# Keys of the last layer: 49 block products for four batches at a time, laid between the heads

## The chip, the core and the metric

The kernel runs on one core of a Trainium2 chip, in float32. A core has a matrix engine (TensorE, PE in the profile; its weight loads are listed as PEld), a vector engine (DVE), an activation engine (ACT), a general engine (POOL), and a queue (SP) from which this kernel issues its DMAs. Matmuls write to PSUM, eight banks of 128 partitions by 512 floats; DVE and ACT read PSUM, POOL doesn't. The metric is the device time of one execution in microseconds: 2974.27 us in the median of three runs before the change (2973.41 to 2974.33).

## The reference

Four layers work on x (8 batches of 112 tokens, 512 channels), with a context of 8 batches of 375 tokens.

```
x = L0(x, ctx)   # one cross-attention, width 512
x = L1(x, ctx)   # RWKV block: time mix with a scan over the 112 tokens, channel mix
x = L2(x, ctx)   # the same form with other weights
x = L3(x, ctx, ctx):
    h = layer_norm(x);  x = x + cross_attention_1(h, ctx)   # 16 heads of 128
    h = layer_norm(x);  x = x + cross_attention_2(h, ctx)
    return x + gelu(layer_norm(x) @ w_fc1 + b_fc1) @ w_fc2 + b_fc2

cross_attention: q = h @ wq + bq;  k = ctx @ wk + bk;  v = ctx @ wv + bv
    k, v = [k; bias_k], [v; bias_v]        # 376 keys per batch
    out = softmax(q k^T / sqrt(128)) v @ wo + bo
```

The change concerns `k = ctx @ wk` of the last layer: 375 tokens of eight batches, 512 channels in, 16 x 128 out, in each of two attentions.

## The kernel before, in words

**Products by seven.** Large products are done by a scheme of seven block products for a 2 x 2 block matrix, where the plain way has eight. It needs sums and differences of the blocks of both factors beforehand and of the products afterwards. The seven are called k1, k2, k5, k6, k7, k8, k9. For the weights the sums are made by POOL (`weight_sums`, L1021 to L1038: four instructions of 512 columns for a 512 x 512 weight). For the context they are made once in layer 0 (`park`) and stored in DRAM as `blocks`: for each pair of batches seven combinations of two batches and two channel halves.

**Values and early keys in the scans.** The values of the last layer don't depend on x, so they are computed during layers 1 and 2, by the generator `values` (L820). It is a sequence of pieces, each a block product of two matmuls with its evacuation; `fill(n)` runs the next n pieces wherever it stands in the code of layers 1 and 2: in layer norms, and once or twice per step of the scan (L688, L697). Four sets of 48 units in all give the values of both attentions; a fifth set of three units (L831) gives the keys of attention 1, groups 1 and 2, batches 0 and 1: 56 matmuls of 125 columns a unit. Results go to DRAM (`store`, L913). Between sets, `relay` (L852) replaces the seven weight blocks step by step, some by DMA, some by POOL, while the last unit of the old set and the first units of the new one run; `after` (L957) lets a step go when a named piece and two more have been made. Inside the scans the order of the instructions of PE, DVE, ACT and POOL is the order in which they are written (`manual_schedule`, L679). Everywhere else, and on the SP queue, a planner orders each engine's instructions by its own costs, in program order where several are ready.

**Channel mix** (`channel_mix`, L720): layer norm, a shifted difference (POOL, L359), two mixed inputs xk and xr (DVE, L738), three projections fk, fr, fv with evacuation by ACT (L753, L763) or DVE (L769), and the addition to x by POOL (L770). In layer 2 the call at L731 runs all pieces that are left.

**The last layer** (`attention`, L1166). The 16 heads are taken in four groups of four. For each group the queries come from a product by seven (`project7`, `seven`, L1047); then for each of eight batches and each head of the group: scores (L1289), softmax (`softmax`, L212: maximum by DVE, exponential by ACT, scaling by DVE at L220), three transposes (L1292), and per batch the product with the values (L1302) and the addition of the bias (L1309). The output projection of the group is again a product by seven. Two PSUM banks (`mm`) hold products, two (`sc`) scores, three transposes, one the context.

**The keys before** (`key_pieces`, `chained`, L1176 and L1105). Before batches 0, 2, 4, 6 of a group the keys of that batch and the next are made: seven products, in two halves of the outputs, each of two accumulating matmuls of 375 columns. That is 28 matmuls and 14 evacuations per pair of batches. They alternate between two banks. Each pair loads its context and four combinations anew. In the first group of an attention the pieces of batches 0 to 3 also fill the layer norm before (`first_keys`, L1206); there the additions are POOL's, elsewhere DVE's (L1140, L1142). Of 32 pairs of batch and group in both attentions, 30 are made so, and two come from the early keys.

**Between groups** four pieces of the output projection, four of the next queries, and the rest follow each other (`some`, L1258).

Of the kernel before, what the change touches and what calls it, by code (L numbers as in the profile page):

```python
# [22 lines left out]
F32 = mybir.dt.float32  # L23
# [6 lines left out]
P = 128  # L30
B, L, C, S = 8, 112, 512, 375
N = B * L
# [16 lines left out]
BLOCK = 2 * CT  # L49

# [58 lines left out]
def tile_kernel(ctx: ExitStack, tc: tile.TileContext, d: dict, out: bass.AP):  # L109
# [14 lines left out]
    def weight(name, g=None):  # L124

        w = wpool.tile([P, NC, C], F32, tag="w", name=f"w_{name}_{g}")
        nc.sync.dma_start(w, d[name] if g is None else d[name][g])
        return w
# [421 lines left out]
    def time_mix(n, pre, center_h, pick, k, v, r, g, decay, rows):  # L550
# [8 lines left out]
        with (  # L559
# [119 lines left out]
            with tc.manual_schedule(engines=ORDERED):  # L679
                vp = led(0)  # L680
                for c in range(NC):
                    side = beside(c)
                    for at, j in enumerate(order):
# [13 lines left out]
                        fill(int(at not in (6, 10)))  # L697
# [22 lines left out]
    def channel_mix(n, pre, names, first):  # L720
        nonlocal filler
        with (
# [11 lines left out]
            def mixed(maa, name):  # L734
                y = one.tile([P, NC, N], F32, name=name)
# [13 lines left out]
            rr = one.tile([P, NC, N], F32, name=f"rr{n}")  # L749
# [6 lines left out]
            xk = mixed(names["fk"], f"xk2_{n}")  # L756
            project(ps, f_k, lambda c, h: halves(xk[:, c, :], h), squared, f"fk{n}")
            xr = mixed(names["fr"], f"xr2_{n}")
# [20 lines left out]
            else:  # L779

                for _ in values_pieces(0):
# [3 lines left out]
                y, sq = (  # L785
                    wpool.tile([P, NC, C], F32, tag="w", name=f"{what}_ln3")[:, :, :NH] for what in ("y", "sq")
# [4 lines left out]
                shared["normed"] = y  # L791

# [27 lines left out]
    def values():  # L820
# [6 lines left out]

        pre = "L3_xattn_"
        pool, spill, ps = shared["pool"], shared["spill"], shared["ps"]
        sets = [("wv", i, (gr, gr + 1)) for i in (1, 2) for gr in (0, 2)] + [("wk", 1, (1, 2))]  # L830
        units = [(at, unit) for at in range(len(sets)) for unit in range(UNITS if at < 4 else 3)]  # L831
# [20 lines left out]
        def relay(at, old, new):  # L852
# [8 lines left out]
            yield "k1"  # L861
            nc.gpsimd.tensor_sub(old["k1"], a11, a21)
            yield "k5"
            nc.gpsimd.tensor_add(a21, a21, a22)
            yield "k9"
            nc.gpsimd.tensor_sub(old["k6"], a21, a11)
            yield "k7"
            raw(old["k7"], at, 0, 1)
            yield "k8"
            raw(old["k8"], at, 1, 1)  # L870
            yield "k5"
            raw(old["k5"], at, 0, 0)
            new["k1"] = old["k5"]
            yield "k6"
            nc.gpsimd.tensor_sub(old["k2"], old["k7"], old["k6"])
            yield "k9"
            nc.gpsimd.tensor_copy(old["k9"], a21)
# [19 lines left out]
        def product(p, t, s, start=True):  # L897

            if len(p.shape) == 2:
                todo = [(p, t[k], s[:, k], k) for k in range(2)]  # L900
            else:
                todo = [(p[:, o], s[:, k, o * P : (o + 1) * P], t[k][:, :CT], k) for o in range(HG) for k in range(2)]

            for n, (to, left, right, k) in enumerate(todo):
                nc.tensor.matmul(to, left, right, start=start and n == 0, stop=k == 1, skip_group_check=True)  # L905

        def shaped(y, f):
# [602 lines left out]
```

## Time and profile before

| what | us |
|---|---|
| median of three runs | 2974.27 |
| the profiled execution | 2975.13 |
| its span, first to last instruction | 2972.9 |
| PE busy | 2865.5 |
| DVE, ACT, POOL busy | 1608.9, 999.1, 876.6 |

The mean granted clock of PE was 0.986. In time: layer 0 to about 160 us, layer 1 to 790 (its scan from 363), layer 2 to 1441 (its scan from 982), attention 1 to about 2094, attention 2 to 2790, then the MLP. "Busy" is the time in which an engine runs at least one instruction. In a group's line "<-" stands between the tile that is written and those that are read; "[1.30 <-ACT k L1136]" behind a timeline row says that the engine was idle for 1.30 us before it, and that ACT's instruction on line 1136 ended that. A float32 matmul is recorded as two passes, so it counts as two.

### The profile page before, as it was taken

What the parts mean: (1) busy time and instruction counts of PE and PEld (TensorE: products, weight loads), DVE (VectorE), ACT (ScalarE), POOL (GpSimd) and SP (SyncE); (2) the same over time, 40 slices, a digit from 0 to 9 for tenths busy, and PEclk for the clock granted to TensorE, in tenths of its full rate; (3) what the DMA queues carried; (4) which work ended last, traced back from release to release, by engine and by line L of the source; (5) the groups of instructions that cost most, each with busy time, mean ns of one, the idle gap of its engine ahead of it and who ended that gap; (6) DMA issues with size and microseconds to landing.
All of it is one profiled execution on the core that took longest, in us unless ns stands there. A gap on an engine that the chain in (4) does not pass through costs nothing.

```text
span 2972.9 us, 29802 instructions
## 1 busy us (share of the span) xinstructions
PE 2865.5 (96%) x10130; PEld 1561.6 (53%) x10130; DVE 1608.9 (54%) x2350; ACT 999.1 (34%) x1992; POOL 876.6 (29%) x702
## 2 busy tenths in 40 slices
PE   8989999999999999999899999999999999999999
PEld 4734443344444433356466666666565666656544
DVE  1563288857342687743445454545555454545455
ACT  2123355533233455532332222223331323323311
POOL 2142078754231587732411010100302010000030
PEclk9989999999999999999999999999999999999999
DMA  7421398944321888742344343334233433432110
GB/s 255 150 89 45 116 294 248 275 135 127 95 66 57 254 244 263 225 143 70 130 125 133 118 139 114 122 109 149 88 114 100 151 107 119 140 104 87 39 57 25
DMA packets 199318, 402.90 MB, mean 136 GB/s; under 512 B 33288, under 2 KB 119592, under 8 KB 192384
## 3 DMA queue, kind: packets, MB, share of 16 engines
q1 hardware_dynamic: 199168, 401.01, 43.1%
q8 instruction: 81, 1.33, 0.2%
q14 instruction: 69, 0.57, 0.1%
HBM read 323.16 MB, written 77.91 MB: 135 GB/s over the span
## 4 chain that ended last, share of the span: by engine, by line
PE 80%; DVE 8%; POOL 4%; DMA 3%; ACT 3%; issue 2%; SPq 0%; DVEq 0%; POOLq 0%; ACTq 0%
PE ps_vk L905 13%; PE ps_k1k L1133 10%; PE ps_k5k L1133 7%; PE av L1302 6%; PE sc L1289 5%; PE ps_o L161 3%; PE pt L1292 3%; PE ps_k1q L1060 2%; PE ps_r L484 2%; PE ps_k L484 2%; PE ps_k5q L1060 2%; PE ps_fr L161 2%; PE ps_k7q L1060 2%; PE ps_fk L161 2%; PE ps_k7fc L1060 1%
## 5 line engine op out<-in xcount | busy, mean ns | idle before, releaser
L905 PE MATMUL ps_vk<-wv,cv 128*128 128x512 f32 x1336 | 602.9, 602 | 31.4 <-DMA wv<-in_L_xattn_wv 12.7
L905 PEld LDWEIGHTS ps_vk<-wv,cv 128*128 128x128 f32 x1336 | 251.4, 192 | 366.9 <-issue 306.9
L931 POOL TENSOR_TENSOR k<-k,k 128x512 f32<-128x512 f32 (+1 forms) x153 | 202.1, 1321 | 308.1 <-ACT k L930 261.3
L691 DVE TENSOR_TENSOR_SCAN st<-decay,kv 128x904 f32<-128x904 f32 x128 | 260.7, 2037 | 16.5 <-POOL rs L695 3.8
L695 POOL TENSOR_TENSOR rs<-st,r 128x896 f32<-128x896 f32 x128 | 246.6, 1927 | 55.6 <-DVE st L691 46.6
L218 ACT ACTIVATE prob<-sc,top 112x376 f32<-112x376 f32 (+1 forms) x264 | 151.8, 575 | 322.8 <-DVE top L215 195.3
L1289 PE MATMUL sc<-k,q 128*112 128x376 f32 x512 | 201.1, 485 | 0.7 <-ACT prob L218 0.7
L1302 PEld LDWEIGHTS av<-pts,v 125*128 125x128 f32 (+1 forms) x1536 | 185.0, 193 | 31.4 <-DVE pts L1298 16.3
L1282 POOL COPY k<-over_k 128x4 f32<-128x4 f32 x64 | 13.8, 224 | 604.7 <-PE sc L1289 576.7
L1302 PE MATMUL av<-pts,v 125*128 125x112 f32 (+1 forms) x1536 | 189.1, 277 | 2.1 <-DVE pts L1298 2.0
L1133 PE MATMUL ps_k1k<-cs,wsk 128*128 128x375 f32 x480 | 179.8, 483 | 1.5 <-ACT p1k L1136 1.5
L687 DVE TENSOR_TENSOR kv<-vp,k 128x904 f32<-128x904 f32 x128 | 141.5, 1105 | 70.3 <-ACT vp L589 64.8
L215 DVE TENSOR_REDUCE top<-sc 112x1 f32<-112x376 f32 (+1 forms) x264 | 143.4, 544 | 64.4 <-PE sc L1289 51.9
L930 ACT COPY k<-ps_vk 128x512 f32<-128x512 f32 (+1 forms) x153 | 89.2, 583 | 183.1 <-PE ps_vk L905 180.1
L998 ACT COPY k<-ps_vk 128x512 f32<-128x512 f32 (+1 forms) x153 | 89.1, 582 | 157.6 <-PE ps_vk L905 151.7
L1292 PEld LDWEIGHTS pt<-ident_l,prob 112*125 112x125 f32 (+1 forms) x768 | 97.9, 176 | 73.0 <-DVE prob L220 43.9
L1292 PE MATMUL pt<-ident_l,prob 112*125 112x112 f32 (+1 forms) x768 | 121.2, 277 | 3.3 <-DVE prob L220 2.1
L220 DVE TENSOR_SCALAR prob<-prob,total 112x376 f32<-112x376 f32 (+1 forms) x264 | 118.3, 449 | 8.0
L1133 PEld LDWEIGHTS ps_k1k<-cs,wsk 128*128 128x128 f32 x480 | 90.0, 191 | 60.1 <-issue 2.4
L1140 DVE TENSOR_TENSOR k<-ps_k5k,u2k 128x375 f32<-128x375 f32 x52 | 28.5, 549 | 159.2 <-PE ps_k5k L1133 158.2
L589 ACT COPY vp<-vj 128x896 f32<-128x896 f32 x124 | 112.8, 910 | 4.4 <-DMA vj<-rows 0.4
L1309 DVE TENSOR_TENSOR ctxt<-av,bv 128x448 f32<-128x448 f32 x64 | 40.0, 625 | 128.3 <-PE av L1302 128.2
(384 smaller groups left out, 4792.2 us busy)
## 6 DMA issues: line engine op xcount, KB each, us to landing
vj<-rows SPq DMA_DIRECT2D x124, 448.0 KB
cv<-blocks SPq DMA_DIRECT2D x181, 251.5 KB
cs<-blocks SPq DMA_DIRECT2D x120, 375.0 KB
wvs<-k SPq DMA_DIRECT2D x128, 256.0 KB
v<-wvs SPq DMA_DIRECT2D x64, 512.0 KB
cx<-in_ctxT SPq DMA_DIRECT2D x38, 750.0 KB
v<-wvs SPq DMA_DIRECT2D x64, 252.0 KB
wvs<-k SPq DMA_DIRECT2D x64, 224.0 KB
```

What stands on the lines that cost most here:

```text
L161: nc.tensor.matmul(p, w[:, k, o * P : (o + 1) * P], rhs(k, h), start=k == 0, stop=k == NC - 1)
L215: nc.vector.tensor_reduce(top, scores, AX.X, ALU.max, negate=True)
L218: nc.scalar.activation(prob, scores, AF.Exp, bias=top, accum_out=total)
L691: nc.vector.tensor_tensor_scan(flat(st), flat(decay[:, c]), flat(kv), 0.0, ALU.mult, ALU.add)
L695: nc.gpsimd.tensor_mul(by_batch(rs), st[:, :, :L], by_batch(r[:, c, :]))
L905: nc.tensor.matmul(to, left, right, start=start and n == 0, stop=k == 1, skip_group_check=True)
L931: nc.gpsimd.tensor_add(y, z, y)
L1060: nc.tensor.matmul(to, lhsT, rhs, start=start and k == 0, stop=k == 1, skip_group_check=not start)
L1133: nc.tensor.matmul(y, lhsT, rhs, start=start and k == 0, stop=k == 1, skip_group_check=True)
L1289: nc.tensor.matmul(sc, q[:, o, tok], kt[:, o, :], start=True, stop=True)
L1292: nc.tensor.transpose(pt[t][:nt, o, :], prob[:, t0 : t0 + nt], ident[:L, :L])
L1302: nc.tensor.matmul(av[:, o, :], v[:nt, t, o * HD : (o + 1) * HD], pts[:nt, t, o, :], start=t == 0, stop=t == 2,)
```

## The change

1. The fifth set of `values` goes; its sets hold values alone. In `relay` each step now names its own lag: three loads are issued right after the piece that frees their slot, and the first weight moves to its final slot a piece of the next unit later. In the scan of layer 2 four instead of two steps in sixteen run one piece fewer.
2. In the channel mix of layers 1 and 2 a new function `finer` makes, for four batches each, the 49 combinations of context blocks that two levels of the scheme need, and stores them in DRAM (128 x 375 floats each). rr takes xk's buffer.
3. The keys of a group are made for four batches ("quad") at a time by 49 products of one 128 x 128 weight block and one combination of 375 columns. Seven inner products of one outer product accumulate in two banks: k1, k6, k7, k8 in one, k2, k5, k9 in the other, each evacuated before the next of that bank. At the start of an attention, two outer products go side by side over four banks. The weight's combinations take 16 POOL instructions per group. Each product loads its combination, seven ahead, into eight buffers. The adds from PSUM are DVE's, copies ACT's, adds between SBUF tiles POOL's.
4. The pieces lie between the heads: three after each head of batches 0 to 3 (the second quad of the group), and 0, 3, 5, 5 after each head of batches 4 to 7 (the first quad of the next group). The last group has none in batches 4 to 7. In the layer norms before an attention, 4 + 8 + 8 + 10 pieces (attention 1, one half) or 4 + 5 + 5 + 6 (attention 2, each half) are run, and the rest of the 49 before the queries.
5. The context of a group takes the queries' buffer. Weights of the last layer rotate over three tiles, a fourth holds the key weight's outer sums. The output projection and the next queries follow each other whole.

```diff
+SEVEN = dict(k1=0, k6=2, k2=5, k7=4, k5=1, k8=6, k9=3)
+INNER = ("k1", "k2", "k6", "k7", "k5", "k8", "k9")
...
+    def weight3(name, g):
+        shared["turn"] = turn = (shared.get("turn", -1) + 1) % 3
+        w = shared["w3"][turn]
+        nc.sync.dma_start(w, d[name][g])
+        return w
...
-                        fill(int(at not in (6, 10)))
+                        fill(int(at not in ((6, 10) if n == 1 else (2, 6, 10, 14))))
...
+            finer(n - 1, one)
...
+    def finer(quad, pool):
+        for e, (what, pos) in enumerate(SEVEN.items()):
...
+                nc.sync.dma_start(y.rearrange("p c k s -> p c (k s)"), from_[:, :, :BLOCK])
...
+            t = pool.tile([P, BLOCKS, S], F32, tag="finer", name=f"finer{quad}_{e}", bufs=1)
...
+            for what, y in (("k1", b11), ("k2", b21), ("k9", b22)):
+                nc.scalar.copy(to[what], y)
+            nc.gpsimd.tensor_sub(to["k5"], b12, b11)
+            nc.gpsimd.tensor_sub(to["k6"], b22, to["k5"])
+            nc.gpsimd.tensor_sub(to["k7"], b22, b12)
+            nc.gpsimd.tensor_sub(to["k8"], b21, to["k6"])
+            at = (quad * BLOCKS + e) * BLOCKS * S
+            nc.sync.dma_start(shared["finer"][:, at : at + BLOCKS * S], t.rearrange("p j s -> p (j s)"))
...
-        sets = [("wv", i, (gr, gr + 1)) for i in (1, 2) for gr in (0, 2)] + [("wk", 1, (1, 2))]
+        sets = [("wv", i, (gr, gr + 1)) for i in (1, 2) for gr in (0, 2)]
...
-            yield "k1"
+            yield "k1", 2
             nc.gpsimd.tensor_sub(old["k1"], a11, a21)
-            yield "k5"
+            yield "k5", 2
             nc.gpsimd.tensor_add(a21, a21, a22)
-            yield "k9"
+            yield "k7", 0
+            raw(old["k7"], at, 0, 1)
+            yield "k2", 0
             nc.gpsimd.tensor_sub(old["k6"], a21, a11)
-            yield "k7"
-            raw(old["k7"], at, 0, 1)
-            yield "k8"
+            yield "k8", 0
             raw(old["k8"], at, 1, 1)
-            yield "k5"
+            yield "k5", 0
             raw(old["k5"], at, 0, 0)
+            yield "k6", 2
+            nc.gpsimd.tensor_sub(old["k2"], old["k7"], old["k6"])
+            yield "k2", 0
+            nc.gpsimd.tensor_copy(old["k9"], a21)
+            yield "k1", 0
             new["k1"] = old["k5"]
-            yield "k6"
-            nc.gpsimd.tensor_sub(old["k2"], old["k7"], old["k6"])
-            yield "k9"
-            nc.gpsimd.tensor_copy(old["k9"], a21)
...
+        def key_pieces(gr, quad, block, more_banks=None):
...
+            kts = [keys.tile([P, HG, T], F32, tag="kt", name=f"k{u}_{j}", bufs=7) for j in range(4)]
+            together = [("k1", "k6"), ("k2", "k7"), ("k5", "k8"), ("k9",)] if more_banks else [(e,) for e in SEVEN]
+            todo = [(e, f) for es in together for f in INNER for e in es]
...
+                    tokens[m] = near.tile([P, S], F32, tag="t2", name=f"t2_{u}_{m}", bufs=8)
+                    nc.sync.dma_start(tokens[m], shared["finer"][:, at : at + S])
...
+                p = banks[e][int(f in ("k2", "k5", "k9"))]
+                nc.tensor.matmul(
+                    p, block(e, f), tokens[m], start=f in ("k1", "k2", "k5"), stop=True, skip_group_check=True
+                )
+                yield
+                y = at(to, *inner[f])
+                if p is banks[e][1] or base == to:
+                    nc.vector.tensor_add(y, p, y)
+                else:
+                    nc.scalar.copy(y, p)
...
+                                nc.gpsimd.tensor_add(y, y, at(add, half, o))
...
+                fills = (8, 8, 10) if i == 1 else (5, 5, 6)
+                layer_norm_half(ps, work, halves(h_in, h), h, *scales, f"ln3_{i}", room, ln_bank, fills)
+        fill(BLOCKS * BLOCKS)
...
-            ctxt = keep.tile([P, HG, N], F32, tag="ctxt", name=f"ctxt{i}_{gr}")
+            ctxt = q
...
+                if b == 0:
+                    filler = key_pieces(gr, 1, block)
+                    following, pieces_of = next(filler), (3, 3, 3, 3)
+                elif b == BH and gr < NG - 1:
+                    block = key_weight(gr + 1)
+                    filler = key_pieces(gr + 1, 0, block)
+                    following, pieces_of = next(filler), (0, 3, 5, 5)
...
+                    fill(pieces_of[b % BH])
+                if b % BH == BH - 1:
+                    fill(BLOCKS * BLOCKS)
+                    kts = following
```

The 49 products of a quad take these places in the keys (`c` names context batch and output half of the outer level; "spare" is a tile of its own):

```diff
+            outer = dict(
+                k1=("c11", None),
+                k6=("c12", "c11"),
+                k2=("c11", "c11"),
+                k7=("c22", "c12"),
+                k5=("spare", None),
+                k8=("c21", "c22"),
+                k9=("c12", "c12"),
+            )
```

## The prediction

> **What bounds the kernel now.** First the busy times of the page, then the windows by stage, which say where TensorE has room, then the timeline of single instructions, for prices.
>
> ```profile
> PE 2865.5 (96%) x10130; PEld 1561.6 (53%) x10130; DVE 1608.9 (54%) x2350; ACT 999.1 (34%) x1992; POOL 876.6 (29%) x702
> ...
> 363.00:612.00 249.00, 239.78 (x718) 98.32 (x717) 209.84 (x138) 142.55 (x264) 197.12 (x125) 0.99 0.92 267
> 982.00:1252.00 270.00, 255.35 (x764) 103.87 (x766) 221.73 (x145) 149.24 (x277) 208.78 (x134) 0.99 0.88 256
> 1310.00:1368.00 58.00, 54.33 (x373) 44.04 (x372) 40.78 (x32) 24.40 (x38) 30.16 (x22) 1.00 0.50 157
> 1660.00:1810.00 150.00, 150.00 (x636) 94.91 (x635) 80.86 (x183) 42.26 (x110) 17.28 (x20) 1.00 0.40 128
> ```
>
> Columns: stretch, its length, busy us of PE, weight loads, DVE, ACT, POOL, the granted clock, DMA share, GB/s. In the last layer (1660 to 1810) PE is never idle; in the scans (363, 982) it is busy 95 to 96%. All idle PE time is 2972.9 - 2865.5 = 107.4 us. So PE work taken out comes off the end, as long as nothing late replaces it.
>
> Prices, from PE's timeline (f32 matmuls are recorded in two passes, so "x4" is two matmuls) and from single rows:
>
> ```profile
> 1667.73 1.43 PE L1133 MATMUL ps_k1k<-cx,w_L_xattn_wk 128*128 128x375 f32 x4
> 1669.00 1.43 PE L1133 MATMUL ps_k5k<-cs,wsk 128*128 128x375 f32 x4
> 1348.39 14.45 PE L905 MATMUL ps_vk<-cv,wv 128*128 128x125 f32 x128
> 1334.04 0.81 SPq L925 DMA_DIRECT2D wks<-k  x2
> 1345.40 11.41 DVE L738 SCALAR_TENSOR_TENSOR xk<-sxc,vecs,xc 128x448 f32<-128x448 f32 x8 [3.46 <-POOL sxc L360]
> 1460.53 0.98 POOL L1142 TENSOR_TENSOR k<-k,u3k 128x375 f32<-128x375 f32 x1 [0.60 <-ACT u3k L1136]
> 1594.79 1.26 POOL L1036 TENSOR_TENSOR wsk<-w_L_xattn_wk 128x512 f32<-128x512 f32 x1
> 1594.74 1.52 DVE L220 TENSOR_SCALAR prob<-prob,total 112x376 f32<-112x376 f32 x1
> 1596.33 0.56 PE L1292 MATMUL pt<-ident_l,prob 112*125 112x112 f32 x3 [0.38 <-DVE prob L220]
> 1473.36 1.53 PE L1133 MATMUL ps_k1k<-cx,w_L_xattn_wk 128*128 128x375 f32 x4 [1.30 <-ACT k L1136]
> 1120.09 2.91 PE L905 MATMUL ps_vk<-wv,cv 128*128 128x512 f32 x4 [3.52 <-DMA wv<-in_L_xattn_wv]
> 1109.11 7.46 PE L905 MATMUL ps_vk<-wv,cv 128*128 128x512 f32 x16 [2.16 <-POOL wv L866]
> ```
>
> Starts 1.27 us apart for two matmuls: 0.632 us per 375-column matmul. 64 matmuls of 125 columns in 14.3 us: 0.223 us. From the chain (26.61 us for 62 records of 512 columns): 0.858 us. A 375-column copy out of PSUM takes 0.47 us on ACT, an add 0.55 on DVE, an SBUF add 0.98 on POOL. The two rows at 1594 show the interplay that matters later: DVE's scaling of the probabilities takes 1.52 us instead of 0.42 while POOL adds, and PE then waits 0.38.
>
> **The change, part by part.** The sum is made against the profiled execution, 2975.1 us (span 2972.9 and 2.2 around it), 0.9 above the median 2974.3.
>
> *1. Early keys leave the scans.* The fifth set (3 units of 56 matmuls) goes: 168 x 0.223 = 37.5 us of PE. It ran from 1319 to 1368, in layer 2's second layer norm. Eight fills leave scan 2, so eight value pieces (two matmuls, 1.716 us) move to where the keys were; the fills then end exactly with the values: 358 - 21 = 337 pieces, taken 169 in layer 1 and 168 in layer 2.
> Scan 2: 8 x 1.716 = 13.7 us off PE. PE would be busy 241.6 us against DVE's 221.7, so PE stays the longer. I take -12; bounds -13.7 and -5 (DVE's order then holds some of it).
> Layer norm: from the end of the output projection (1309.9) to the steady run of the next one (1368.2) are 58.3 us. With 14 pieces (24.0 us) and four mean matmuls (3.0) PE isn't the limit: the norm's chain is. Its first mixed input starts at 1345.4, four at 1.43 us end at 1351, 17 us earlier than 1368. The same stage of layer 1, with 21 pieces, takes 671.1 to 718 = 46.9, which would give -11.4. I take -15, between; bounds -20 and -5.
>
> *2. Weight steps regrouped.* PE waited in the scans 0.23 + 3.52 + 1.00 us for re-laid weights by DMA and 2.68 + 2.16 for POOL's differences. Three loads are now issued two pieces earlier (3.4 us) and the first weight changes slot a unit later; POOL's steps stay at the same pieces. I take -4; bounds -4.8, and +5 if a load that waits at the head of SP's queue for PE holds the scan's row loads and stores behind it.
>
> *3. The 49 token blocks.* Each of two channel mixes gets 14 loads of 375 KB, 7 stores of 1.3 MB, 21 ACT copies (21 x 0.47 = 9.9 us) and 28 POOL differences (28 x 0.98 = 27.4 us). Cover: 118 and some 115 us of channel mix, in which POOL works 43 and 39. With one buffer each, a round is load, differences, store: bound from the 4.1 us of a 251 KB load in the chain and the transfer of 2.1 MB at the scan's 267 GB/s (7.9 us) to about 12 us, 84 in all, so it just fits. What costs is POOL beside the norm's DVE work (the xk row: 1.43 us each instead of 0.67). I take +3 per layer, +6; bounds 0 and +45. If the cover fails, ACT stands at a copy whose load is late, sigmoids queue behind it, and after six full banks (6 x 3 = 18 us) PE stops.
>
> *4. Fewer key matmuls.* Before: 30 pair-groups x 28 = 840; after: 16 quads x 49 = 784. 56 x 0.632 = -35.4 us, all in stretches with PE full. (Groups 1 and 2 of the first attention grow by 8.8 each, the other six shrink by as much.)
>
> *5. What the new form adds in attention.* Per group of about 158 us of PE:
> - evacuations: 98, of them 58 on DVE (31.8 us) and 40 on ACT (18.8); before, 40 ACT copies and about 11 us of DVE adds. DVE rises from 81 to about 102 us, still under PE; a copy that waits for its matmul holds the exponentials (ACT) or maxima (DVE) behind it.
> - POOL: 40 adds (39 us) and 16 weight sums (5632 columns at 1.27 us per 512: 14 us, before 5). POOL goes from 17 to some 64 us per group, 12% to 40% busy. Of 254 scalings seen, 33 met a POOL instruction and took 0.25 us longer; at 40%, 256 x 0.4 x 0.25 = 26 us of DVE instead of 8. PE felt a quarter of it (2.1 us of pt waiting for prob). I take +5; bounds 0 and +26.
> - one bank holds k1, k6, k7, k8: k7 follows k6 in the same bank at once, and must wait for the copy (0.2 + 0.47 + 0.1 = 0.75 us). 16 x 7 = 112 such places, 84 us if PE has nothing else. Between the heads it has scores and transposes, and at each layer's start two products alternate over four banks. Now a piece is two matmuls and such waits sum to about 7 us. I take +6; bounds 0 and +84.
> - the fifth batch of six groups has no pieces while POOL makes weight sums: DVE 7.6 us against PE 6.75, plus blocked scalings: +4 (0 to +18). The last four batches of each attention lose their pieces: +4 (0 to +14).
> - start of each attention: all 49 pieces (31 us) before the first score instead of 20 double ones (25.3), behind 14 us of weight sums and beside layer norm's DVE: +4 (-3 to +15).
> - loads: 98 of 192 KB per group instead of 24 larger ones, 8 MB more: 178 GB/s on average instead of 128. SP issues in about 0.4 us, so 39 us of 158. In a burst 192 KB per 0.632 us are 304 GB/s, about what the scan's share allows (267/0.92 = 290). Seven are issued ahead (4.4 us, the cv load's 4.1). Output and query projections no longer interleave, but the key pieces fill the wait before them. Together +3; bounds 0 and +20.
> At nothing: the context in the queries' buffer (the next queries are written after the output projection's last read, which PE runs first anyway), seven key buffers for eight tiles (the fourth new one waits for the scores of one batch), and three rotating weight tiles instead of four (each 1 MB load has a projection of 21 us ahead of it; a load that is late by its own 6 us would cost that at each of seven group ends, 42 us).
> Together +26, so attention alone -9.4.
>
> Two rules of the Trainium skill stand against this part. "DMA: Bandwidth & Descriptors", section Bandwidth, says to batch loads to a MiB and prices one DMA at about 2 us fixed plus its bytes at 436 GB/s: an estimate of 2.44 us for 192 KB, 0.35 with seven in flight; by it nothing is added unless fewer than four fly. "SBUF — State Buffer", section Who interferes with whom, says a DVE instruction that needs the shared ports blocks fully behind GpSimd: a mean block of half a 0.98 us add would give 256 x 0.4 x 0.49 = 50 us of DVE where the rows give 26.
>
> Sum: -12 - 15 - 4 + 6 - 35.4 + 26 = -34.4; 2975.1 - 34.4 - 0.9 = **2940**.
>
> **Rivals.**
> - *All of it comes through.* For: PE idles nowhere in 1660 to 1810 now, the smaller pieces give the order more to fill with. Against: DVE and POOL both rise. Without the 32 us of costs and with both layer-2 stages at their best: 2974 - 33.7 - 4 - 35.4 = 2901.
> - *The copy between k6 and k7 sets the pace (slower).* Place: each product's third and fourth piece; price 0.75 us each, 84 in all. For: the row at 1473, where PE waited 1.30 for a copy. Against: scores in between. Savings without this term are 40.4, so it decides from 40.4/84 = 48% uncovered; at three quarters 2974 - 40 + 63 = 2997.
> - *DVE becomes the bound.* Softmax, 58 adds, and POOL's blocks at their upper ends (+26, +18, +14 for 13 taken): 2940 + 45 = 2985, and half of that 2963.
> - *The token blocks hold ACT.* Parts 1 and 3 collide, +45 for +6: 2979.
>
> **How the numbers follow.** Forecast 0.46 (its own range 2914 to 2965), all through 0.14, k6 to k7 0.20, DVE 0.11, token blocks 0.09. A difference of 0.2% (6 us) is about what can be told from none. Faster: 0.45 + 0.14 + 0.03 + 0.02 = 0.64; same 0.01 + 0.01 + 0.03 + 0.03 = 0.08; slower 0.19 + 0.05 + 0.04 = 0.28. The range, 2893 to 3000, leaves out the upper part of the k6 case and less at the bottom.
>
> **What the new profile would show.** PE busy near 2793 (72.9 less) and idle time near 145 us; 1568 key records; no 125-column L905 group in the layer norm; POOL near 1290; scalings longer in the mean than 0.45. Wrong if PE waits for ACT or DVE copies of keys exceed 40 us, if the sigmoids wait for token-block copies, or if PE waits for key loads.

## The result, and the profile after

The changed kernel takes 2986.14 us in the median of five runs (2983.25 to 2990.73), where the kernel before, in the same comparison, takes 2974.20 (2970.27 to 2974.33). The ratio is 1.0044, with a 95% interval of 1.0033 to 1.0056: 13 us slower, where 34 us faster was forecast. The profiled execution is the longest of the five (2990.7, span 2989.0), so its stages are compared one by one and not by their sum.

The page of the changed kernel, busy times:

```profile
PE 2831.4 (95%) x9682; PEld 1498.1 (50%) x9682; DVE 1813.2 (61%) x2658; ACT 997.7 (33%) x2017; POOL 1270.7 (43%) x1136
```

PE works 34 us less than before (2865.5), not 73 less; PE's idle time is 2989.0 - 2831.4 = 157.6 us, before 107.4. DVE has 204 us more, POOL 394. The windows that answer to those of before: the first scan, the second, layer 2's second norm from the output projection to the steady run of the next one, and one steady group of attention 1 (before, its groups took 149.4 us with early keys and 167.4 without):

```profile
365.30:614.30 249.00, 240.01 (x719) 98.61 (x719) 210.41 (x138) 142.92 (x265) 197.65 (x125) 0.99 0.92 268
990.00:1249.00 259.00, 244.16 (x735) 99.46 (x736) 221.41 (x147) 145.54 (x269) 203.82 (x130) 0.98 0.89 262
1306.60:1356.00 49.40, 36.72 (x77) 14.18 (x76) 33.62 (x23) 21.88 (x38) 31.76 (x27) 0.90 0.56 185
1680.60:1846.90 166.30, 162.38 (x663) 98.98 (x662) 108.70 (x223) 45.57 (x118) 65.13 (x72) 1.00 0.56 170
```

The norm is 9 us shorter. The group of attention is the surprise. Its PE work can be counted from the kernel before: 167.4 us with 112 key matmuls is 167.4 - 112 x 0.632 = 96.6 us of everything else; with 98 it should take 96.6 + 61.9 = 158.5. It takes 166.3, in every full group of both attentions (the distance of the same bias addition from group to group is 165.8 to 166.9). So 8 us are lost in a group, 64 in eight, while PE's idle time shows 3.9 in this one.

Stage lengths, from the first matmul of one product to the first of the next in PE's records (the scan counts from its first product `ps_y`, the queries from their first k6 product; the last line ends with the last matmul of the output projection):

| stage | before | after | difference |
|---|---|---|---|
| layer 0 to the first value piece | 166.8 | 170.1 | +3.3 |
| that to layer 1's fr | 573.2 | 573.7 | +0.5 |
| fr to the scan of layer 2 | 269.7 | 273.6 | +4.0 |
| scan of layer 2 to its output projection | 276.0 | 266.4 | -9.6 |
| output projection to layer 2's fr | 104.3 | 93.1 | -11.2 |
| fr to the queries of attention 1 | 98.7 | 105.5 | +6.8 |
| both attentions, to the last output projection | 1301.1 | 1323.2 | +22.1 |

The first line is drift from run to run: that start lies between 162.7 and 170.1 us in the runs of this study, whatever the kernel.

What PE waited for in the attentions (us in total, times, longest), first before, then after:

```profile
PE ps_k5k L1133 <- ACT k L1136: 2.5, 3, 1.3
PE pt L1292 <- DVE prob L220: 2.1, 4, 1.2
```

```profile
PE pt L1345 <- DVE prob L231: 21.6, 34, 2.0
PE ps_k5k_k L1237 <- DVE spare L1243: 3.9, 6, 0.6
PE ps_k1k_k L1237 <- ACT k L1245: 2.9, 6, 0.5
...
PE ps_k5k_k L1237 <- DVE k L1243: 2.1, 7, 0.4
```

The transposes wait for the scaled probabilities, 21.6 us against 2.1. The group of scalings in the last layer (busy, mean ns of one, idle before), before and after:

```profile
L220 DVE TENSOR_SCALAR prob<-prob,total 112x376 f32<-112x376 f32 x256 | 115.0, 450 | 7.7
```

```profile
L231 DVE TENSOR_SCALAR prob<-prob,total 112x376 f32<-112x376 f32 x256 | 160.8, 629 | 6.2
```

One place from the timeline of the changed kernel shows how, DVE, POOL and PE in this order:

```profile
1701.41 0.16 DVE L230 RECIPROCAL total<-total 112x1 f32<-112x1 f32 x1
1701.61 1.10 DVE L231 TENSOR_SCALAR prob<-prob,total 112x376 f32<-112x376 f32 x1
...
1704.10 0.42 DVE L231 TENSOR_SCALAR prob<-prob,total 112x376 f32<-112x376 f32 x1
```

```profile
1701.52 0.98 POOL L1254 TENSOR_TENSOR k<-k,spare 128x375 f32<-128x375 f32 x1 [0.82 <-DVE spare L1243]
```

```profile
1701.19 0.79 PE L1342 MATMUL sc<-k,q 128*112 128x376 f32 x2
1701.91 0.90 PE L1237 MATMUL ps_k1k_k<-t,w 128*128 128x375 f32 x2
1702.77 0.56 PE L1345 MATMUL pt<-ident_l,prob 112*125 112x112 f32 x3
```

The POOL add ends at 1702.50; the scaling that began beside it ends 0.21 us later and took 1.10 us. The next, alone, took 0.42. Of the 256 scalings 136 met a POOL instruction and took 0.82 in the mean, the other 120 took 0.41; before, 36 met one. The 95 of them over 0.6 us that met POOL end 0.21 us behind a POOL instruction (0.211 to 0.215 for the middle eight tenths). PE's three rows show a second thing: the key product starts at 1701.91, 0.72 behind the score where 0.63 is usual, and its record is 0.90 long where 0.79 is usual; the transposes start 0.86 behind it, 0.23 more than usual. No row has an idle mark, since the records overlap. So part of what PE loses stands in its busy time.

From here on "lost" is worked out so: the distance from the start of each pass to the next, less the usual one (0.316 us for 375 columns, 0.376 for 448, 0.112 for a value product, 0.104 for a transpose), summed where it is over 0.05. In the second group of attention 1 this gives 2.2 us before, none of it ahead of key products; after, 10.2, of it 5.4 ahead of key products and 4.4 ahead of transposes. The difference is the 8 us.

### The profile page after: what moved, and what is told of

Same layout as the page of the kernel before. It is cut to its first block, busy times and chain, and to the rows that moved or that the text cites. A ratio compares the mean times of both kernels' runs of the same rounds, so it can differ in the third digit from the quotient of the medians.

```text
span 2989.0 us, 31590 instructions
## 1 busy us (share of the span) xinstructions
PE 2831.4 (95%) x9682; PEld 1498.1 (50%) x9682; DVE 1813.2 (61%) x2658; ACT 997.7 (33%) x2017; POOL 1270.7 (43%) x1136
## 4 chain that ended last, share of the span: by engine, by line
PE 71%; DVE 15%; POOL 5%; ACT 3%; issue 3%; DMA 3%; SPq 0%; DVEq 0%; POOLq 0%; ACTq 0%
PE ps_vk L936 12%; PE ps_k1k_k L1237 7%; PE av L1359 5%; PE ps_k5k_k L1237 5%; PE sc L1342 4%; PE ps_o L172 3%; PE pt L1345 2%; DVE prob L231 2%; DVE st L702 2%; PE ps_r L495 2%; PE ps_k L495 2%; PE ps_k5q L1081 2%; PE ps_fr L172 2%; PE ps_k7q L1081 2%; PE ps_k1q L1081 2%
## 5 line engine op out<-in xcount | busy, mean ns | idle before, releaser
L959 POOL TENSOR_TENSOR k<-k,k 128x512 f32<-128x512 f32 x144 | 188.2, 1308 | 266.0 <-ACT k L958 196.6
L702 DVE TENSOR_TENSOR_SCAN st<-decay,kv 128x904 f32<-128x904 f32 x128 | 260.8, 2037 | 21.6 <-POOL rs L706 8.9
L1237 PE MATMUL ps_k1k_k<-t,w 128*128 128x375 f32 x640 | 265.9, 500 | 7.8 <-ACT k L1245 3.4
L1237 PE MATMUL ps_k5k_k<-t,w 128*128 128x375 f32 x544 | 219.2, 488 | 6.7 <-DVE spare L1243 3.9
L1245 ACT COPY k<-ps_k1k_k 128x375 f32<-128x375 f32 x256 | 120.0, 470 | 259.9 <-PE ps_k1k_k L1237 259.0
L1254 POOL TENSOR_TENSOR k<-k,k 128x375 f32<-128x375 f32 x128 | 127.7, 1001 | 184.0 <-DVE k L1243 137.1
L1243 DVE TENSOR_TENSOR k<-ps_k5k_k,k 128x375 f32<-128x375 f32 x288 | 156.3, 545 | 72.0 <-PE ps_k5k_k L1237 58.5
L231 DVE TENSOR_SCALAR prob<-prob,total 112x376 f32<-112x376 f32 (+1 forms) x264 | 164.9, 625 | 6.5
L1345 PE MATMUL pt<-ident_l,prob 112*125 112x112 f32 (+1 forms) x768 | 132.6, 276 | 22.8 <-DVE prob L231 21.6
L1237 PEld LDWEIGHTS ps_k1k_k<-t,w 128*128 128x128 f32 x640 | 105.6, 190 | 94.6 <-ACT k L1245 40.2
L1254 POOL TENSOR_TENSOR k<-k,spare 128x375 f32<-128x375 f32 x128 | 121.3, 954 | 70.1 <-DVE spare L1243 59.1
L958 ACT COPY k<-ps_vk 128x512 f32<-128x512 f32 x144 | 84.0, 583 | 173.1 <-PE ps_vk L936 168.5
```

The costliest lines, as they stand in the source:

```text
L231: nc.vector.tensor_scalar(prob, prob, total, None, ALU.mult)
L702: nc.vector.tensor_tensor_scan(flat(st), flat(decay[:, c]), flat(kv), 0.0, ALU.mult, ALU.add)
L959: nc.gpsimd.tensor_add(y, z, y)
L1237: nc.tensor.matmul(p, block(e, f), tokens[m], start=f in ("k1", "k2", "k5"), stop=True, skip_group_check=True)
L1243: nc.vector.tensor_add(y, p, y)
L1254: nc.gpsimd.tensor_add(y, y, at(add, half, o))
```

## The experiments

The theories: **ports**, POOL's adds hold DVE's scalings and PE gets its probabilities late; **banks**, key products wait for the evacuation of their two PSUM banks; **DVE's load**, its key adds make the softmax late whatever POOL does. For the rest of the change: what the scan part and the block combinations are worth by themselves. Each ratio is to the kernel before on the same chip; differences in us are differences of ratios times 2970.

### Runs 1 to 4: who holds the scalings

Runs 1 and 4 have this edit, on the changed kernel and on the kernel before:

```diff
-        nc.vector.tensor_scalar(prob, prob, total, None, ALU.mult)
+        nc.scalar.mul(prob, prob, total)
```

> The changed kernel with one edit: the probabilities are scaled by ACT instead of DVE (256 in the last layer, 8 in layer 0). In the changed kernel PE loses about 8 us in each of the eight groups of attention beyond its matmuls: 4.4 around the transposes, which wait for scaled probabilities, and 5.4 around key products, less the 2 that the kernel before had. Theory 'ports' (POOL's adds hold DVE's scalings: mean 0.625 us for 0.449 before): the transposes' part goes, and the part of the key products that wait for DVE with it; 2950 to 2960 us. Theory 'banks' (key products wait for their two PSUM banks whoever scales): at most 5 us gained, 2980 to 2990. Theory 'DVE's load' (DVE has 109 of 166 us per group, 82 before): gains like 'ports' here; the next two kernels tell them apart.

Run 2 moves POOL's adds of key tiles to DVE:

```diff
-                                nc.gpsimd.tensor_add(y, y, at(add, half, o))
+                                nc.vector.tensor_add(y, y, at(add, half, o))
```

> The changed kernel with POOL's 320 adds of key tiles done by DVE (0.55 us each for 0.98). Theory 'ports': POOL meets few scalings, their mean falls to about 0.45 and the waits of the transposes fall from 4.4 to about 1.5 us a group; DVE gains 22 - 7 = 15 us a group, still under PE: 2955 to 2980. Theory 'DVE's load': DVE at some 124 of 166 us makes the softmax later: 2995 to 3020. Theory 'banks': no change from this, 2980 to 2990.

Run 3 leaves them out, so that its keys lack part of their sums:

```diff
-                    for dst, add in later:
+                    for dst, add in later[:0]:
```

> The changed kernel without the 320 adds of key tiles by POOL (left out: so the keys lack part of their sums). Theory 'ports': scalings at 0.45 us in the mean, transposes wait 1.5 us a group for 4.4, and the start of attention 1, where POOL's adds stand in the chain from 1450 to 1473, is some 5 us shorter: 2945 to 2965. Theory 'DVE's load': its work is the same but for the blocked time, 2975 to 2985. Theory 'banks': 2980 to 2990.

> The kernel before with the probabilities scaled by ACT: the control for the first run. There PE waits only 2.1 us for scaled probabilities. Theory 'ports': within 4 us of the kernel before, 2970 to 2976. If it gains as much as the changed kernel does, the gain is of the engine and not of the conflict with POOL.

Measured: run 1 2959.4 us, ratio 0.9960 (0.9946 to 0.9975), 25 us below the changed kernel. Run 2 2966.6, 0.9985 (0.9974 to 0.9997), 18 below, though DVE now works 1896 us. Run 3 2947.1, 0.9921 (0.9905 to 0.9937), 37 below. Run 4 2976.6, 1.0028 (1.0016 to 1.0039), 8 us *slower* than the kernel before, where at most 4 were expected: on ACT a scaling takes 0.61 us for 0.41, so where POOL is out of the way the move costs. POOL doesn't lengthen it: 117 scalings of run 1 that met POOL took 0.607, the others 0.610.

Waits of PE and the scalings of run 3:

```profile
PE pt L1345 <- DVE prob L231: 11.3, 19, 2.0
PE sc L1342 <- ACT prob L229: 2.6, 3, 1.5
```

```profile
L231 DVE TENSOR_SCALAR prob<-prob,total 112x376 f32<-112x376 f32 x256 | 126.7, 495 | 6.3
```

No key wait stands among the first rows any more, though by the distances 3.3 to 4.1 us a group are still lost ahead of key products. "Banks" and "DVE's load" fall as the whole explanation: run 2 adds to DVE's load and gains. The adds of POOL cost 37 of the 64 us. Run 3 also shortens the keys' own way; the meeting of adds and scalings by itself is read from run 1, where the adds stay: 25 us, with the longer scaling on ACT already paid for. A reservation for all these runs: the planner orders the instructions anew for each kernel, and what of a difference is the new order was not separated.

### Runs 5, 6, 11 and 15: fewer POOL adds, and a better version

Run 5 adds the base tile while the product leaves PSUM:

```diff
+                folded = base is not None and base != to and not (more_banks and e == "k6")
                 if p is banks[e][1] or base == to:
                     nc.vector.tensor_add(y, p, y)
+                elif folded:
+                    nc.vector.tensor_add(y, p, at(base, *inner[f]))
                 else:
                     nc.scalar.copy(y, p)
...
-                    later = [(to, base)] if base is not None and base != to else []
+                    later = [(to, base)] if base is not None and base != to and not folded else []
```

> The changed kernel with the sums of k6, k7 and k8 folded into the evacuation: DVE adds the product in PSUM to the base tile in one step, where ACT copied (0.47 us) and POOL added later (0.98 us). Per group 24 POOL adds and 24 ACT copies fewer, 24 DVE adds (0.55 us) more; at the starts of attentions k6 stays as it is. Theory 'ports': POOL keeps 16 of 40 adds, so about half of what moving all 40 to DVE gave, and DVE has less to do than there (13 us a group for 22): 2955 to 2970, a little under the second run's 2967. Theory 'DVE's load': slower than the changed kernel's 2986.

Run 6 has this and the scaling on ACT:

> The fold, and the probabilities scaled by ACT: POOL's remaining adds then meet no scalings, and ACT has 24 copies fewer. If conflicts with POOL are the main loss and the rest is lateness of DVE, this is the best of the four: 2945 to 2957. If ACT's longer softmax chain costs what the folding gains, it stays at the first run's 2959.

Run 11 drops POOL's last key adds between the heads too (k5 goes from PSUM to both its places, k8 before it):

```diff
+                if e == "k5":
+                    y = at("c22", *inner[f])
+                    nc.vector.tensor_add(y, p, y)
+                    y = at("c12", *inner[f])
+                    nc.vector.tensor_add(y, p, y)
```

> As the sixth run (k6, k7, k8 folded, scaling by ACT), and k5 is added by DVE straight from PSUM to both of its places, k8 before k5: 16 POOL adds and 8 ACT copies a group fewer, 22 DVE adds more. In the sixth run the groups take 159.5 us where their matmuls need 158.5, so at most 1 us a group is to be had: 2932 to 2940. If DVE at some 120 of 159 us is late, or the banks are held too long, 2945 to 2965.

Run 15 is run 6 without the fold at the starts of the attentions:

```diff
-                folded = base is not None and base != to and not (more_banks and e == "k6")
+                folded = base is not None and base != to and not more_banks
```

> As the sixth run (fold and scaling by ACT, 2940 us), with the fold only in the pieces between the heads, not at the starts of the attentions. There the fold puts adds on DVE beside the layer norm: the stretch between the attentions took 99.5 us with it and 93 to 95 without. If that is so, 4 to 6 us less: 2934 to 2937. If the 99.5 is of another order of the pieces, 2940.

Measured: run 5 2954.7 us, 0.9950 (0.9936 to 0.9965). Run 6 2940.3, 0.9900 (0.9875 to 0.9926). Run 11 2962.5, 0.9967 (0.9956 to 0.9978). Run 15 2937.0, 0.9884 (0.9862 to 0.9907): 34 us faster than the kernel before and 48 faster than the changed kernel. One steady group of run 15 (columns as in the windows above), and the busy times of its page:

```profile
1666.30:1825.70 159.40, 159.38 (x661) 98.88 (x661) 100.12 (x214) 53.05 (x126) 40.82 (x48) 1.00 0.57 178
```

```profile
PE 2811.7 (96%) x9682; PEld 1501.4 (51%) x9682; DVE 1741.5 (59%) x2562; ACT 1072.6 (37%) x2113; POOL 1096.9 (37%) x968
```

The group takes 159.4 us where its matmuls were counted at 158.5: 7 of the 8 us are back. The group still loses 3.5 us by the distances, 2.3 of it ahead of key products. Run 6 came out better than expected. Run 15 differs from it where that was expected: from the last bias addition of attention 1 to the first of attention 2, 93.1 us for 99.5 (the two times' intervals overlap).

Run 11 is the miss. With POOL at 27 us a group and DVE at 118 (both summed over instructions) it lost 20 us against run 6. The first row of PE's waits in its attentions:

```profile
PE ps_k1k_k L1235 <- DVE k L1245: 11.6, 15, 5.0
```

Key products now wait for DVE, which reads the same bank twice for k5. Taking all adds from POOL is too much; the best of these versions leaves it 16 a group. Per group, second of attention 1, in us (the number of meetings is of both attentions):

| kernel | group | lost ahead of keys | lost ahead of transposes | scalings that met POOL, mean | ratio |
|---|---|---|---|---|---|
| changed | 166.3 | 5.4 | 4.4 | 136, 0.82 | 1.0044 |
| run 1, ACT scales | 163.1 | 5.5 | 1.3 | 117, 0.61 | 0.9960 |
| run 2, adds on DVE | 164.3 | 5.6 | 2.2 | 57, 0.78 | 0.9985 |
| run 3, adds left out | 161.7 | 4.1 | 1.5 | 51, 0.83 | 0.9921 |
| run 5, fold | 161.6 | 4.2 | 1.1 | 99, 0.75 | 0.9950 |
| run 6, fold, ACT scales | 159.4 | 2.4 | 0.7 | 97, 0.60 | 0.9900 |
| run 11, no key adds on POOL, ACT scales | 161.9 | 4.3 | 0.7 | 52, 0.61 | 0.9967 |
| run 15, fold between heads, ACT scales | 159.4 | 2.3 | 0.8 | 97, 0.60 | 0.9884 |

The key products' part doesn't fall when the scalings alone move (5.5), and falls when DVE is relieved of them *and* POOL's adds become fewer (2.4). That points to lateness of the evacuations for 3 of the 5.4 us; the 2.4 that stay, where the kernel before lost nothing, were not explained further.

### Runs 7, 8, 10, 12 and 14: the rest of the change

Run 7 is the kernel before with the scan part:

```diff
-        sets = [("wv", i, (gr, gr + 1)) for i in (1, 2) for gr in (0, 2)] + [("wk", 1, (1, 2))]
+        sets = [("wv", i, (gr, gr + 1)) for i in (1, 2) for gr in (0, 2)]
...
-                        fill(int(at not in (6, 10)))
+                        fill(int(at not in ((6, 10) if n == 1 else (2, 6, 10, 14))))
```

with `relay` and `after` as in the change.

> The kernel before with the scan part of the change alone: no fifth set, four steps in sixteen with one piece fewer in the second scan, weight steps regrouped. The two pairs of keys that came early are made in attention instead, 56 matmuls at 0.632 us = 35.4 us. By my sum the scans and the layer norm give back 12 + 15 + 4 = 31: +4 to the kernel before, 2974 to 2982. By the traces of the changed kernel (scan 2 shorter by 9 to 11, the stage of layer 2's channel mix by 11): 35.4 - 21 = +14, 2984 to 2990. Rival, the stage was shorter because finer took POOL's or ACT's time elsewhere: no number.

Run 8 has `finer` and its calls alone, run 10 both parts:

> The kernel before with the combinations of context blocks of the change made and stored, and not used. My sum has +3 for each of two layers, +6. The traces show +4 to +5 from layer 1's projections to the scan of layer 2, and up to +6 between layer 2's channel mix and the first queries: +6 to +11, 2976 to 2985 where the kernel before has 2970 to 2974. Rival: it is hidden and the differences in the traces come from the weights' loads and the starts of attention: 0 to +2.

> The kernel before with the scan part and the combinations of blocks, so with everything of the change but the new keys. The scan part alone gave +3 to its kernel before, the combinations alone +14. In the traces, of those 14 five lie behind layer 1's projections and nine in layer 2's norm, where the early keys stood; with the early keys gone I expect +8 for the combinations: +11, 2980. Then what the new keys cost in attention, beyond their 112 matmuls fewer than here (70.8 us), is 2986 - 2980 + 71 = some 77 us. Rival: the two parts just add, +17, 2986.

Run 12 is run 6 with the differences on DVE, run 14 is run 10 with loads and stores only:

```diff
-            nc.gpsimd.tensor_sub(to["k5"], b12, b11)
+            nc.vector.tensor_sub(to["k5"], b12, b11)
```

```diff
+        t = pool.tile([P, BLOCKS, S], F32, tag="finer", name=f"finer{quad}", bufs=1)
+        nc.gpsimd.memset(t, 0.0)
...
-            nc.gpsimd.tensor_sub(to["k5"], b12, b11)
```

> As the sixth run, and the 56 differences of the block combinations are made by DVE (0.55 us) instead of POOL (0.98). If the combinations cost their 8 us because POOL's work slows DVE's mixed inputs, which stood at 13 us for eight rows in layer 1 where a row of its own takes 0.67, most of it comes back: 2932 to 2937. If it is the stores and loads or the ACT copies, no change, 2940; if DVE's own queue is what is late there, slower, 2942 to 2950.

> As the tenth run (scan part and block combinations on the kernel before, 2985 us), but the combinations aren't computed: 14 loads and 7 stores per layer stay, the 21 copies and 28 differences are left out, and zeros are stored. If the loads and stores cost the 11 to 14 us: 2985. If the copies on ACT or the waiting for them costs: 2972 to 2975, as with the scan part alone.

Measured: run 7 2971.7 us, 1.0011 (0.9997 to 1.0025), +3. It makes 56 key matmuls more, 35.4 us, so the scan part gives 32. Run 8 2982.5, 1.0046 (1.0029 to 1.0063), +14. Run 10 2985.1, 1.0046 (1.0031 to 1.0061), +14, so the combinations cost 10 beside the scan part and 14 by themselves; the intervals don't tell these apart, and my +11 for run 10 is inside its interval. Run 12 2941.0, 0.9893 (0.9876 to 0.9909): as run 6. Run 14 2978.7, 1.0026 (1.0015 to 1.0036): between.

DVE's eight rows of layer 1's second mixed input beside POOL's differences in the changed kernel (13.22 us in run 6), and without them in run 12:

```profile
723.87 13.23 DVE L749 SCALAR_TENSOR_TENSOR xr<-sxc,vecs,xc 128x448 f32<-128x448 f32 x8
```

```profile
718.70 6.86 DVE L749 SCALAR_TENSOR_TENSOR xr<-sxc,vecs,xc 128x448 f32<-128x448 f32 x8
```

The conflict is gone, 6.4 us of DVE are saved, and the kernel is no faster: in layer 1 the matmuls before xr had not ended. DVE makes the 56 differences there, so a gain elsewhere that this work cancels is not excluded. PE's waits at the start of layer 2 in run 14, with the loads and stores alone, are these:

```profile
PE ps_t L451 <- DVE xx L442: 2.9, 3, 2.1
...
PE ps_ruk L542 <- DVE ruk L533: 2.3, 1, 2.3
PE mean_ln L186 <- issue: 1.2, 1, 1.2
```

Run 7 has 1.4, none and none there. Where layer 2 begins late can be read from DVE's rows. First run 7, then run 14: the last evacuation of fv, and the subtraction that opens layer 2's first norm.

```profile
789.53 0.62 DVE L769 TENSOR_TENSOR rr<-ps_fv,rr 128x448 f32<-128x448 f32 x1 [2.38 <-PE ps_fv L161]
791.39 2.02 DVE L187 TENSOR_TENSOR xa<-x,mean_ln 128x1792 f32<-128x1792 f32 x1 [1.24 <-POOL x L770]
```

```profile
784.09 0.62 DVE L774 TENSOR_TENSOR rr<-ps_fv,rr 128x448 f32<-128x448 f32 x1 [2.38 <-PE ps_fv L165]
...
789.61 2.02 DVE L191 TENSOR_TENSOR xa<-x,mean_ln 128x1792 f32<-128x1792 f32 x1
```

In run 7 they start 1.9 us apart, in run 14 5.5. Between them run 14 has the three sums for the mean and the first copies of re-laid weights, which run 7 made among the evacuations of fv and earlier. All five kernels of this study without the combinations have 1.9, all twelve with them 5.5. So 3.7 us come from where these instructions stand, in run 14 too, where nothing is computed; why they stand there (the planner's choice, or buffers and loads that come later) was not separated. A second part is in layer 2's norm: from the output projection to fr run 7 takes 89.4 us, run 14 89.7, run 10 93.2, so 3.8 us come with the copies and differences. Over the whole, run 14 has some 4 us of run 10's 10, but the intervals are as wide as that.

### Runs 9 and 13: POOL's adds on the kernel before

Both put 40 adds of 375 columns per group behind the heads of the kernel before, on a tile `scr` that nothing reads. Run 9 adds the tile to itself:

```diff
+                    for _ in range(2 if o == 3 else 1):
+                        nc.gpsimd.tensor_add(scr, scr, scr)
```

> The kernel before with 40 POOL adds of 375 columns per group that nothing needs, one behind each head and a second one behind each fourth (their result is not used). If the conflict of POOL's adds with DVE's scalings costs by itself what leaving the adds out of the changed kernel gave back (39 us), this kernel is that much slower: about 3010. If the conflict costs only because DVE has 58 key adds a group more in the changed kernel and its softmax comes too late, the kernel before has room for it (DVE 87 of 150 to 167 us): 2972 to 2985, with the scalings that meet POOL still near 0.7 us.

Run 13 reads the batch's keys:

```diff
+                    for _ in range(2 if 2 <= b < 7 else 0):
+                        nc.gpsimd.tensor_add(scr, scr, kt[:, o, :S])
```

> The kernel before with 40 POOL adds of 375 columns per group, eight for each of batches 2 to 6, that read the keys of their batch and so can't run ahead (their result is not used). If POOL's adds cost 5 us a group by meeting the scalings alone: about 3010. If it takes DVE's added key adds too: 2972 to 2985, with scalings that meet POOL at 0.7 us or more and a mean above 0.55.

Run 9 took 3147.7 us, 1.0598, and answers nothing about the scalings: the adds depended on nothing, so they ran ahead: all 320 lie between 1370 and 1697 us, around the start of attention 1, and held what POOL does there. Two single waits of PE say so:

```profile
PE mean_ln L182 <- DVE part_mean_ln L180: 67.1, 1, 67.1
PE sc L1292 <- POOL k L1138: 56.5, 1, 56.5
```

Its later groups, without adds, were as before (150.3 us). Run 13 took 2994.5 us, 1.0082 (1.0060 to 1.0105), +24, between the two expectations. PE's wait for probabilities and the group of scalings of run 13:

```profile
PE pt L1295 <- DVE prob L220: 18.5, 47, 1.7
```

```profile
L220 DVE TENSOR_SCALAR prob<-prob,total 112x376 f32<-112x376 f32 x256 | 151.1, 590 | 7.8
```

142 scalings met POOL, at 0.73. The second group lost 3.7 us more than before, all of it ahead of transposes. So 320 POOL adds cost 24 us without the new keys, in a kernel whose DVE is busy 55% of the span; beside the new keys the same number cost 37 (run 3). What the other 13 are was not separated: the adds stand at other places, and run 3 shortens the keys' way too.

## Why the prediction was wrong

| term of the sum | forecast, us | measured, us | from |
|---|---|---|---|
| 1, 2: early keys leave, weight steps | -31 | -32 | run 7: +3, less 35.4 |
| 3: token blocks | +6 | +10 to +14 | runs 8 and 10 |
| 4: fewer key matmuls | -35.4 | -35.4 | 1568 records, as forecast |
| 5: the new form in attention | +26 | +66 to +70 | what is left of +13 |

- **Parts 1 and 2** held: the scan and the norm are 9.6 and 11.2 us shorter in the profiled execution (12 and 15 forecast), and in run 7, where no combinations disturb, 14.0 and 14.8. The regrouping did less than the 4 taken: in the second scan PE's 4.5 us for loaded weights are gone, but PE waits 5.0 for the same POOL difference for which it waited 2.2.
- **Part 3** had the right sign, and its bounds hold. "What costs is POOL beside the norm's DVE work" isn't borne out: that conflict was there in layer 1, and run 12 took it away for nothing. What the traces show instead are 3.7 us at the start of layer 2 and 3.8 in layer 2's norm. The rival that ACT holds the sigmoids is half right. In the changed kernel they did queue behind copies whose load was late, three at a time. PE did not stop for it: its 64 passes of fr ran unbroken, 24.22 us (ACT, then PE):

```profile
756.28 1.32 ACT L821 COPY finer<-pair 128x375 f32<-128x375 f32 x3 [7.60 <-DMA pair<-blocks]
757.51 1.40 ACT L775 ACTIVATE rr<-ps_fr 128x448 f32<-128x448 f32 x3
```

```profile
743.81 24.22 PE L172 MATMUL ps_fr<-xr,w_L_xattn_fWr_None 128*128 128x448 f32 x64
```

- **Part 4** held by count and by price: passes still start 0.316 us apart.
- **Part 5** is the failure, by some 42 us, enough to turn the sign. The step that failed is the second item, POOL's adds: "PE felt a quarter of it (2.1 us of pt waiting for prob). I take +5; bounds 0 and +26." Leaving the adds out gave 37 us (run 3). Three numbers were too small. I let 40% of the scalings meet POOL, its busy share; 136 of 256 did, 53%, since a scaling meets an add already when it begins up to its own length ahead of it. I took 0.25 us each, from the meetings before; it was 0.41 (0.82 less 0.41). That makes 55 us of DVE, not 26; the group rows say 160.8 - 115.0 = 45.8 more than before. And I let PE feel a quarter, as in a kernel where few scalings were late; in run 13 DVE grew by 151.1 - 115.0 = 36.1 us and the kernel by 24, two thirds. The upper bound took all of DVE's time as PE's and still was below the 37, since the DVE time itself was too low.
- A second term was too small: key products that wait for the evacuation of their bank. The sum has +6 for it, at k6 to k7 alone, and nothing for DVE's and ACT's evacuations elsewhere ("still under PE"). With POOL's adds gone, run 3 still loses 3.3 to 4.1 us a group ahead of key products, some 28 in eight groups, where the kernel before lost none. With the 37 that is 65 of the 66 to 70, so the items taken at +15 together (batches without pieces, starts, loads) are left with little.
- Of the other items in part 5, **k6 to k7** was no problem. With the key matmuls named by their place in the program order, k7 loses 7.0 us in the fourteen quads between the heads (3.3 ahead of its first passes, 3.7 ahead of its second); k2 loses 9.4, k1 8.2, k8 7.4, k6 2.3. In 50 of the 98 outer products the planner put k5 between k6 and k7. So the rival that I gave 0.20 is out (its 84 us for 7.0), though the time ended near it; the 0.75 us behind it is a slip, its terms add to 0.77. **Starts** cost little: +6.8 at the first, where nine matmuls more are 5.7, and 94.6 us between the attentions for 94.5. **Loads**: none of PE's listed waits in the attentions is for a combination.
- The rival "DVE becomes the bound" named 2985, with POOL's blocks at their upper end, and is the nearest in time and in mechanism, but DVE was no bound: it works 109 of 166 us. It was late, not full. That its figure fits to 1 us is luck: it has POOL's blocks at +26, below the 37, and two terms for batches without pieces at +32 that no run measured apart.

On the two rules of the Trainium skill that the prediction weighed. The page "SBUF — State Buffer", section Who interferes with whom, has DVE and GpSimd share a port pair as an exclusive lock; the estimate made from it, 50 us of DVE, is nearer to the 55 measured than the 26 from the rows, and a scaling that ends 0.21 us behind POOL's add is what a lock would look like in a trace. The page "DMA: Bandwidth & Descriptors", section Bandwidth, spoke against many loads of 192 KB; with seven in flight 784 of them cost PE no listed wait here. The fixed 2 us that the prediction took from that page stand in its section Anatomy of one DMA, for DMAs issued by GpSimd, while this kernel issues from SP; no run here measures them.

The signs named ahead: 1568 key records, no 125-column group in the norm, POOL at 1271 (1290 forecast) and scalings above 0.45 in the mean all came. PE busy at 2831, not 2793, was the sign of the failure. Key waits of 16 us in the list stayed under the limit of 40 that I had set, but the list shows only idle time; by the distances the fourteen quads alone lost 34.7.

## What to carry to other kernels

When a change adds work to POOL beside DVE instructions that PE waits for, price every meeting at the time to the end of POOL's instruction, count meetings by overlap and not by POOL's busy share, and expect the matmuls to feel most of it where DVE's result is needed next (two thirds in run 13), though DVE is far from full. The cheap cure is to let the sum happen where the data passes anyway (in the evacuation from PSUM) and to move the scaling to an engine that POOL doesn't hold; without the conflict that same move cost 8 us. Before relieving an engine, see whether its result is what PE waits for: 6.4 us of DVE in layer 1 bought nothing.

## What the runs showed of the hardware

- A DVE scaling from SBUF to SBUF of 112x376 took 0.41 us alone; the long ones that met POOL ended 0.21 us behind a POOL instruction. DVE's key adds with one operand in PSUM took 0.545 us in the mean, whether they met POOL (179 of 435) or not, and ACT's scaling 0.61 either way.
- A key matmul that had to wait is recorded 0.90 us long instead of 0.79 per pair of passes (33 of 33 in two groups), and the gap ahead of it is hidden under the end of the one before. In a group that lost 10.2 us the profile shows 3.9 as idle; distances from start to start show all of it.
- Work without dependencies is not where it is written: 320 adds written behind the heads of both attentions all ran between 1370 and 1697 us, and the kernel took 177 us longer.
